# Logits in four equal pieces and a fixed plan of what runs between the groups of an attention sum

One core of a Trainium2 chip (trn2). The metric is the device time of one execution in microseconds (us), the median of the runs in the chip's fast state. "Slot" is the kernel's unit of work: one tile of 128 nodes in one of two steps. In the views of the profile PE is TensorE (PEld its weight loads), DVE is VectorE, ACT is ScalarE, POOL is GpSimd and SP is the engine that issues most transfers; L625 is line 625 of that kernel. A line `A <- B` among the waits says that A waited for B.

## The reference

Rows `x` (3327 x 256) are normed and rectified to `h`. Two steps then run an attention whose weights are cut to a nucleus (the largest probabilities that together reach 0.9) beside a diffusion over a sparse adjacency matrix; the result is normed again and added to `x`.

```python
R = S + jnp.eye(N); R = R / R.sum(-1, keepdims=True)
for n in range(STEPS):                      # 2
    A = _top_p_attention(Xa, W1, W2, W3)    # softmax(q k^T), cut to top_p, rows sum to 1
    Xf = R @ Xf
    Xa = A @ Xa
    Z = Z + Xf @ U1[n].T + Xa @ U2[n].T
h = X + Z
return (h - mu) / jnp.sqrt(var + LN_EPS) * ln_g + ln_b
```

## The kernel before

It is software-pipelined: in iteration `i`, tile `i-1` is summed with its attention weights, tile `i` gets its threshold (`settle`), tile `i+1` its first estimates (`first`, in step 1 also `second`), tile `i+2` its logits (`weights`). The sum over 26 blocks is done in seven groups; `fill(k)` puts other work between the groups.

```python
def weights(step, t, qT, ms, fill):                    # cut
    w = HALF * P                                       # 1664: two halves of the keys, 64 rows each
    for n, c in enumerate(range(0, w, 512)):           # pieces 512, 512, 512, 128
        if n >= 2: fill()
        wd = min(512, w - c)
        pl = ps_l.tile([P, 2, 512], F32, ...)
        for a in range(2):                             # both halves of the row groups
            PE.matmul(pl[:, a, :wd], qT[p, :], keys[step][p]...[:, c : c + wd], ...)
        # ACT takes exp out of PSUM: one instruction for 512, two for the last piece

def attend(r, xa, dst, n, fill):                       # cut
    eT = turn(0)                                       # 4 transposes on PE, copy eT on ACT
    for k, j0 in enumerate(starts):                    # 7 groups
        nxt = turn(starts[k + 1]) if ... else None
        fill(k)
        for j in ...: PE.matmul(pa, eT[:, j, :], xa[:, j0 + j, :D], ...)
        eT = nxt

def packed(t, over):                                   # cut: lists of adjacency blocks
    pb = ps_t.tile(...); PE.matmul(pb[:, 0, :1], upto, over, ...)
    V.tensor_copy(ls[:, LIST:], pb[:, 0, :1])          # VectorE frees PSUM

def finish(t, y1, xa2):                                # cut: end of step 1
    V.tensor_tensor(y, y1, xa2, ALU.add)
    mean, rstd = mean_rstd(y)                          # stats on VectorE, rstd on POOL (G)
    V.tensor_scalar(y, y, mean, rstd, ALU.subtract, ALU.mult)

for i in ...:                                          # the slot, cut
    settle(step, i, ...)
    qT, ms = project(step, i + 2)
    def fill(k):
        run(work, 2)                                   # diffusion, first step's ends
        if k in (1, 3): next(meas, None)               # first estimates
    attend(...)
    if step == 1: second(...)
    live[step, i + 2] = weights(...)                   # all logits after the sum
    if step == 0: listed(i + 3); packed(i + 2, ...); gathered(i + 1, ...)   # lists last
    else: xg[i + 1] = fetched(vx, i + 1, D)            # 5 gathers, issued by POOL
```

## Time and profile before

| | before |
|---|---|
| median of its fast runs on the chip of the first comparison | 1726.17 us (1721.45 to 1728.4) |
| profiled span | 1725.2 us |
| slot in step 0 while lists are searched (13 slots, the 5th to the 18th) | 34.60 us |
| slot in step 0 after that (8 slots) | 32.82 us |
| slot in step 1 (the last 17) | 26.34 us |

A slot is measured from one start of the nucleus sum's first pass (`w`, L625; L629 after the change, one a slot) to the next. Of the page of before, the busy totals (part 1), then TensorE, VectorE and granted clock in 40 slices (part 2, one digit per 43 us):

```profile
PE 1481.4 (86%) x6923; PEld 1121.1 (65%) x6923; DVE 1272.9 (74%) x3936; ACT 1103.3 (64%) x2836; POOL 769.3 (45%) x1124
...
PE   5766998899998999999999966988898898988985
...
DVE  4249877777777666466557139889999999999993
...
PEclk8657999889988998998999977989998998989988
```

TensorE fills the first half (step 0), VectorE the second (step 1). The clock row reads 8 as often as 9 in step 0. Sums over two stretches of step 0 give it a number. The columns are stretch, length, busy time with count of PE, PEld, DVE, ACT, POOL, then granted clock, DMA share, GB/s:

```profile
300.00:700.00 400.00, 369.96 (x1664) 274.14 (x1661) 282.21 (x947) 250.84 (x633) 178.86 (x236) 0.88 0.38 109
700.00:933.00 233.00, 216.90 (x1035) 164.28 (x1034) 135.86 (x446) 152.34 (x388) 105.09 (x135) 0.93 0.19 52
```

PE is busy for 92 and 93% of the two stretches, but at 0.88 and 0.93 of its clock.

### The profile page before, as it was taken

The page shows a single profiled execution, that of the slowest core. Times are in us where ns is not written, and L with a number is a line of the kernel's source. Part 1 is how long each engine was busy: PE and PEld are TensorE (multiplying, and loading weights), DVE is VectorE, ACT ScalarE, POOL GpSimd, SP SyncE. Part 2 cuts the span into 40 slices and gives each one's busy share as a digit, 9 for nine tenths or more (in the row PEclk, how much of TensorE's full clock was granted, in tenths as well). Part 3 has the DMA queues.
Part 4 walks back from the last instruction along what each step waited for, and adds up shares of the span by engine and source line. Part 5 has one row for each costly group of instructions (what it writes and reads, how often), then busy time and mean ns, then how long its engine had stood idle before and what let it go on. Part 6 is the DMA issues. An engine that isn't in the chain of part 4 may idle for free.

```text
span 1725.2 us, 23597 instructions
## 1 busy us (share of the span) xinstructions
PE 1481.4 (86%) x6923; PEld 1121.1 (65%) x6923; DVE 1272.9 (74%) x3936; ACT 1103.3 (64%) x2836; POOL 769.3 (45%) x1124
## 2 busy tenths in 40 slices
PE   5766998899998999999999966988898898988985
PEld 4634666667666776776777834666676676766765
DVE  4249877777777666466557139889999999999993
ACT  5376665566566656756765387577686776777751
POOL 6541334543444345435535183456543443436421
PEclk8657999889988998998999977989998998989988
DMA  7541444444444411212212230021221221212210
GB/s 218 152 133 47 125 133 119 129 134 136 119 129 131 113 47 51 63 41 56 58 47 62 59 107 16 21 65 44 71 65 52 65 61 53 71 48 67 71 46 12
DMA packets 86458, 139.62 MB, mean 81 GB/s; under 512 B 14737, under 2 KB 49296, under 8 KB 86320
## 3 DMA queue, kind: packets, MB, share of 16 engines
q1 hardware_dynamic: 67168, 93.76, 17.8%
q0 software_dynamic: 16640, 42.69, 9.6%
q10 hardware_dynamic: 2512, 1.57, 0.3%
q8 instruction: 57, 0.93, 0.2%
q14 instruction: 81, 0.66, 0.1%
HBM read 114.10 MB, written 23.87 MB: 80 GB/s over the span
## 4 chain that ended last, share of the span: by engine, by line
DVE 49%; PE 29%; ACT 11%; issue 4%; DMA 2%; POOL 2%; another core or an unknown queue 1%; SPq 0%; POOLq 0%; ACTq 0%; DVEq 0%
DVE cand L629 12%; PE pa L695 11%; DVE w L625 10%; DVE e L646 6%; DVE jv L594 5%; PE pt L685 5%; DVE cand L636 4%; DVE bb L634 4%; PE pl L526 3%; ACT ja L565 3%; PE pz L778 2%; DVE fm L707 2%; ACT eT L687 1%; DMA at<-in_adj 1%
## 5 line engine op out<-in xcount | busy, mean ns | idle before, releaser
L695 PE MATMUL pa<-x,eT 128*128 128x256 f32 x1352 | 359.4, 404 | 0.0
L687 ACT COPY eT<-pt 128x512 f32<-128x512 f32 (+1 forms) x364 | 198.5, 551 | 240.4 <-PE pt L685 185.1
L526 PE MATMUL pl<-k,qT 64*128 64x512 f32 (+1 forms) x832 | 257.2, 647 | 98.0 <-ACT e L530 78.4
L695 PE MATMUL pa<-xw,eT 128*128 128x256 f32 x1352 | 329.7, 389 | 5.7 <-ACT eT L687 5.7
L565 ACT ACTIVATE ja<-e,g 128x3328 uint8<-128x3328 f32 x104 | 319.6, 3073 | 0.0
L695 PEld LDWEIGHTS pa<-x,eT 128*128 128x128 f32 x1352 | 269.0, 205 | 40.2 <-ACT eT L687 0.2
L695 PEld LDWEIGHTS pa<-xw,eT 128*128 128x128 f32 x1352 | 251.0, 194 | 48.3 <-ACT eT L687 16.1
L685 PE MATMUL pt<-ident,e 128*128 128x128 f32 x1352 | 237.6, 303 | 38.0 <-DVE e L646 25.3
L685 PEld LDWEIGHTS pt<-ident,e 128*128 128x128 f32 x1352 | 183.1, 155 | 106.5 <-DVE e L646 29.9
L629 DVE MAX8 cand<-w 128x8 f32<-128x168 f32 (+1 forms) x1040 | 250.1, 315 | 0.6
L526 PEld LDWEIGHTS pl<-k,qT 64*128 64x128 f32 x832 | 91.3, 220 | 225.7 <-ACT e L530 117.4
L625 DVE SCALAR_TENSOR_TENSOR w<-e,g 128x3328 f32<-128x3328 f32 x52 | 194.7, 3743 | 1.5
L646 DVE SCALAR_TENSOR_TENSOR e<-e,rec 128x3328 f32<-128x3328 f32 x52 | 191.7, 3686 | 4.4 <-DVE rec L644 3.3
L756 POOL DMA_INDIRECT xg<-hx,index x130 | 158.9, 1223 | 79.7 <-PE pr L764 48.6
L530 ACT ACTIVATE e<-pl 128x1024 f32<-128x1024 f32 x156 | 158.3, 1018 | 34.0 <-PE pl L526 33.2
L756 POOL DMA_INDIRECT xg<-vx,index x130 | 154.2, 1186 | 41.6 <-issue 40.9
L707 DVE TENSOR_REDUCE fm<-at 128x4 f32<-128x512 f32 (+1 forms) x182 | 115.5, 639 | 72.9 <-DMA at<-in_adj 72.5
L764 PE MATMUL pr<-xg,ac 128*128 128x257 f32 (+1 forms) x520 | 149.8, 407 | 7.7 <-DMA xg<-hx,index 3.6
L746 POOL DMA_INDIRECT ac<-in_adj,index x130 | 123.8, 953 | 50.5 <-issue 37.4
L473 POOL TENSOR_TENSOR gsum<-gsum,gt 64x65 f32<-64x65 f32 x52 | 16.7, 320 | 267.1 <-ACT gt L472 266.8
L440 POOL TENSOR_SCALAR rstd<-mv 128x1 f32<-128x1 f32 x52 | 21.5, 416 | 211.6 <-DVE g L606 135.8
L764 PEld LDWEIGHTS pr<-xg,ac 128*128 128x128 f32 x520 | 98.3, 209 | 22.5 <-issue 7.0
(200 smaller groups left out, 2212.9 us busy)
## 6 DMA issues: line engine op xcount, KB each, us to landing
at<-in_adj SPq DMA_DIRECT2D x156, 256.0 KB
cx<-ac SPq DMA_DIRECT2D x26, 384.0 KB
ac<-cx SPq DMA_DIRECT2D x26, 384.0 KB
hx<-x SPq DMA_DIRECT2D x26, 128.5 KB
x<-in_x SPq DMA_DIRECT2D x13, 256.0 KB
at<-in_adj SPq DMA_DIRECT2D x26, 128.0 KB
xr<-in_x SPq DMA_DIRECT2D x26, 128.0 KB
vx<-sv SPq DMA_DIRECT2D x26, 128.0 KB
```

Of the source, the lines that this page charges most:

```text
L526: PE.matmul(pl[:, a, :wd], qT[p, :], keys[step][p].rearrange("p a b -> p (a b)")[:, c : c + wd], start=True, stop=True)
L530: S.activation(e.rearrange("p (a n) -> p a n", a=2)[:, :, c : c + wd], pl[:, :, :wd], AF.Exp, accum_out=za[:, n : n + 1])
L565: S.activation(ja, e, f, bias=col(9), scale=-1.0, accum_out=oa[:, k : k + 1])
L625: V.scalar_tensor_tensor(w, e, col(16), e, ALU.is_lt, ALU.mult, accum_out=d2)
L629: V.max(cand[:, 8 * s : 8 * s + 8], w[:, s * SEG : min(NP, (s + 1) * SEG)])
L646: V.scalar_tensor_tensor(e, e, at(1), e, ALU.is_ge, ALU.mult, accum_out=ra)
L685: PE.transpose(pt[:, j, :], e[:, (j0 + j) * P : (j0 + j + 1) * P], ident)
L687: S.copy(eT[:, :w, :], pt[:, :w, :])
L695: PE.matmul(pa, eT[:, j, :], xa[:, j0 + j, :D], start=j0 + j == 0, stop=j0 + j == NT - 1)
L707: V.tensor_reduce(fm[:, j0 : j0 + n], at[:, :n], AX.X, ALU.max, apply_absolute_value=True)
L756: G.indirect_dma_start(out=xg[:, k, :w], out_offset=None, in_=rows, in_offset=bass.IndirectOffsetOnAxis(ap=index[:, t, k : k + 1], axis=0))
L764: PE.matmul(pr[:, :w], ac[:, k, :], own if k == KT - 1 else xg[:, k, :w], start=k == 0, stop=k == KT - 1)
```

## The change

The intent: keep TensorE supplied with matmuls whose results nobody needs at once. The logits come in four equal pieces, and each piece, each list matmul and each part of the first step's ends stands at a fixed place between the groups of the sum. The two list matmuls leave PSUM (the matmul results' memory) by ACT and no longer by VectorE.

```diff
+CUT = 4
-    def weights(step, t, qT, ms, fill):
+    def weights(step, t, live):
+        qT, ms = project(step, t)
+        yield
-        for n, c in enumerate(range(0, w, 512)):
-            if n >= 2:
-                fill()
-            wd = min(512, w - c)
+        wd = w // CUT
+        for n in range(CUT):
+            c = n * wd
...                                       # a yield after each piece
-        V.tensor_copy(ls[:, LIST:], pb[:, 0, :1])
+        S.copy(ls[:, LIST:], pb[:, 0, :1])
...
+        lo = small.tile([P, n + 1], F32, tag="lo", name="lo", bufs=2)
+        S.copy(lo, po[:, 0, : n + 1])     # VectorE then reads lo instead of po
...
+    PLAN = (("wmsss", "lsss", "ewl", "mweel", "weel", "wee", "ee"),    # step 0
+            ("wms", "lss", "w", "mw", "ws", "wss", ""))                # step 1
+            # m: first estimates, w: project, then a piece of logits, s: diffusion,
+            # e: ends of step 0, l: lists (step 0) or load and gathers (step 1)
             def fill(k):
-                run(work, 2)
-                if k in (1, 3):
-                    next(meas, None)
+                for c in PLAN[step][k]:
+                    next(work[c], None)
-            run(meas, 3)
-            if step == 1 and valid(i + 1):
-                second(live[step, i + 1])
+            for c in "mwsel":
+                run(work[c], 99)
+                if c == "m" and step == 1 and valid(i + 1):
+                    second(live[step, i + 1])
```

More of the change, by code (lines that the diff above doesn't have):

```diff
@@ L512, in project @@
         return qT, ms
-    def weights(step, t, qT, ms, fill):
+    def weights(step, t, live):
+        qT, ms = project(step, t)
+        yield
         e = epool.tile([P, NP], F32, tag="e", name="e")
-        za = small.tile([P, 5], F32, tag="za", name="za")
+        za = small.tile([P, CUT + 1], F32, tag="za", name="za")
         G.memset(e[:, N:NP], 0.0)
         w = HALF * P
-        for n, c in enumerate(range(0, w, 512)):
-            if n >= 2:
-                fill()
-            wd = min(512, w - c)
+        wd = w // CUT
+        for n in range(CUT):
+            c = n * wd
             pl = ps_l.tile([P, 2, 512], F32, tag="pl", name="pl")
@@ L528, in weights @@
                           start=True, stop=True)
-            if wd == 512:
+            if n < CUT - 1:
                 S.activation(e.rearrange("p (a n) -> p a n", a=2)[:, :, c : c + wd], pl[:, :, :wd],
                              AF.Exp, accum_out=za[:, n : n + 1])
+                yield
             else:
-                S.activation(e[:, c : c + wd], pl[:, 0, :wd], AF.Exp, accum_out=za[:, 3:4])
-                S.activation(e[:, w + c : N], pl[:, 1, : wd - 1], AF.Exp, accum_out=za[:, 4:5])
+                S.activation(e[:, c:w], pl[:, 0, :wd], AF.Exp, accum_out=za[:, n : n + 1])
+                S.activation(e[:, w + c : N], pl[:, 1, : wd - 1], AF.Exp, accum_out=za[:, n + 1 :])
         g = small.tile([P, 20], F32, tag="g", name="g")
@@ L555, in weights @@
             S.activation(col(10), col(9), AF.Identity, scale=col(5), bias=con(0))
-        return dict(e=e, g=g, col=col, Z=Z)
+        live[step, t] = dict(e=e, g=g, col=col, Z=Z)
     def first(step, r):
@@ L735, in gathered @@
         PE.matmul(po[:, 0, : n + 1], oh, ls[:, DIRECT:], start=True, stop=True)
+        lo = small.tile([P, n + 1], F32, tag="lo", name="lo", bufs=2)
+        S.copy(lo, po[:, 0, : n + 1])
         nth = small.tile([P, 1], F32, tag="nth", name="nth")
-        V.tensor_scalar(nth, po[:, 0, n : n + 1], -1.0, part, ALU.mult, ALU.add)
+        V.tensor_scalar(nth, lo[:, n:], -1.0, part, ALU.mult, ALU.add)
         of = small.tile([P, LIST], F32, tag="of", name="of", bufs=2)
-        V.scalar_tensor_tensor(of[:, :n], place[:, :n], nth, po[:, 0, :n], ALU.is_equal, ALU.mult, accum_out=nth)
+        V.scalar_tensor_tensor(of[:, :n], place[:, :n], nth, lo[:, :n], ALU.is_equal, ALU.mult, accum_out=nth)
         V.tensor_scalar(index[:, t, DIRECT:], nth, -1.0, float(NONE), ALU.mult, ALU.add)
@@ L833, in run, with spread @@
             next(work, None)
-    def side(step, t):
-        if step == 0 and valid(t - 1):
-            yield from first_end(t - 1, *live.pop(("r", t - 1)))
-            yield
-        if not valid(t):
-            return
+    def spread(step, t):
         rr = rrs[:, t : t + 1]
@@ L858, in side, with index_next, refetch @@
         live["f", t] = s1
+    def index_next(t):
+        if valid(t + 3):
+            over[t + 3] = listed(t + 3)
+        yield
+        if valid(t + 2):
+            oh[t + 2] = packed(t + 2, over.pop(t + 2))
+        yield
+        if valid(t + 1):
+            ac[t + 1] = gathered(t + 1, oh.pop(t + 1))
+            xg[t + 1] = fetched(hx, t + 1, D + 1)
+    def refetch(t):
+        if valid(t + 1):
+            ac[t + 1] = adjp.tile([P, KT, P], F32, tag="ac", name="ac", bufs=2)
+            nc.sync.dma_start(ac[t + 1].rearrange("p k r -> p (k r)"), cx[t + 1])
+            xg[t + 1] = fetched(vx, t + 1, D)
+        yield
+    PLAN = (("wmsss", "lsss", "ewl", "mweel", "weel", "wee", "ee"),
+            ("wms", "lss", "w", "mw", "ws", "wss", ""))
     for step in range(2):
@@ L862, in guess_graph_layer @@
         for i in range(-3, NT + (1 if step else 2)):
+            none = iter(())
+            t = i - 1
             if valid(i):
                 settle(step, i, live[step, i])
-            meas = first(step, live[step, i + 1]) if valid(i + 1) else iter(())
-            if valid(i + 2):
-                qT, ms = project(step, i + 2)
-            t = i - 1
-            work = side(step, t) if valid(t) or t == NT else iter(())
+            work = dict(
+                m=first(step, live[step, i + 1]) if valid(i + 1) else none,
+                w=weights(step, i + 2, live) if valid(i + 2) else none,
+                s=spread(step, t) if valid(t) else none,
+                e=first_end(t - 1, *live.pop(("r", t - 1))) if step == 0 and valid(t - 1) else none,
+                l=index_next(i) if step == 0 else refetch(i),
+            )
             def fill(k):
-                run(work, 2)
-                if k in (1, 3):
-                    next(meas, None)
+                for c in PLAN[step][k]:
+                    next(work[c], None)
             if valid(t):
@@ L882, in guess_graph_layer @@
                 del live[step, t]
-            run(meas, 3)
-            if step == 1 and valid(i + 1):
-                second(live[step, i + 1])
-            if valid(i + 2):
-                live[step, i + 2] = weights(step, i + 2, qT, ms, lambda: run(work, 1))
-            run(work, 99)
+            for c in "mwsel":
+                run(work[c], 99)
+                if c == "m" and step == 1 and valid(i + 1):
+                    second(live[step, i + 1])
             if valid(t):
@@ L893, in guess_graph_layer @@
                     finish(t, live.pop(("f", t)), xa)
-            if step == 0:
-                if valid(i + 3):
-                    over[i + 3] = listed(i + 3)
-                if valid(i + 2):
-                    oh[i + 2] = packed(i + 2, over.pop(i + 2))
-                if valid(i + 1):
-                    ac[i + 1] = gathered(i + 1, oh.pop(i + 1))
-                    xg[i + 1] = fetched(hx, i + 1, D + 1)
-            elif valid(i + 1):
-                ac[i + 1] = adjp.tile([P, KT, P], F32, tag="ac", name="ac", bufs=2)
-                nc.sync.dma_start(ac[i + 1].rearrange("p k r -> p (k r)"), cx[i + 1])
-                xg[i + 1] = fetched(vx, i + 1, D)
         prove(step)
```

## The prediction

> **What bounds the kernel now.** I read the page's busy shares first, then the spacing of one instruction that runs once a slot, then sums over stretches inside one slot, then the timeline of TensorE where it stands idle, then the waits.
>
> The program is two steps of 26 slots; one slot handles one tile of 128 nodes. The instruction L625 (first pass of the nucleus sum on VectorE) runs once a slot, so its starts clock the slots. In the timeline they stand at 154.0 us (step 0, third slot) and 933.1 us (the last of step 0), 23 slots in 779 us. The first 15 of these take 34.4 us each: there VectorE also searches the adjacency for the lists (L707), about 11 tiles a slot. The last 8 take 32.8 us. In step 1 nearly all take 26.4 us (1201.3 to 1675.7).
>
> Step 0 is TensorE's. The sums over stretches of one slot (704.1 to 736.0) show how it loses time; columns are stretch, length, busy time and count of PE, PEld, DVE, ACT, POOL, then the granted clock, DMA share and GB/s:
>
> ```profile
> 704.10:713.30 9.20, 9.18 (x44) 6.69 (x42) 9.10 (x27) 2.63 (x5) 2.70 (x5) 1.00 0.08 21
> 713.30:717.10 3.80, 1.75 (x12) 1.36 (x13) 3.56 (x19) 1.81 (x9) 2.88 (x4) 1.00 0.20 52
> 717.10:722.00 4.90, 4.89 (x17) 3.33 (x18) 4.83 (x10) 3.84 (x19) 4.41 (x4) 0.65 0.26 70
> 722.00:736.00 14.00, 14.00 (x76) 11.30 (x75) 1.83 (x11) 12.83 (x25) 5.25 (x10) 1.00 0.22 71
> ```
>
> PE is full except for 3.8 us in which it is idle for 2.05 us; in the 4.9 us after that the clock granted is 0.65, which costs (1 - 0.65) x 4.9 = 1.7 us more. The timeline of PE there:
>
> ```profile
> 713.64 0.49 PE L526 MATMUL pl<-k,qT 64*128 64x128 f32 x4 [0.36 <-issue]
> 714.06 0.38 PE L724 MATMUL pb<-over,upto 128*128 128x1 f32 x2
> 714.30 0.37 PE L735 MATMUL po<-lists,oh 128*128 128x13 f32 x2
> 716.35 0.48 PE L492 MATMUL pq<-qry,w2d 64*128 64x128 f32 x2 [1.67 <-DVE lists L725]
> ...
> 717.67 1.46 PE L526 MATMUL pl<-k,qT 64*128 64x512 f32 x2
> ...
> 722.89 1.12 PE L526 MATMUL pl<-k,qT 64*128 64x512 f32 x2
> ```
>
> The list matmuls pb and po take both buffers of the PSUM pool for transposes. VectorE frees pb by a copy of 0.14 us (L725), but that copy stands behind eight-maximum rounds in VectorE's queue, so the next user (pq) waits 1.67 us. Also, the two halves of one logits piece (L526) are issued 5 us apart: one half alone takes 1.12 us at full clock, while four such pairs issued together (711.29, eight instructions) take 1.99 us.
>
> What a slot costs when nothing stands in its way is seen in the drain of step 0, where two attention slots run without logits, projection and lists:
>
> ```profile
> 940.80:961.70 20.90, 20.90 (x113) 18.06 (x112) 13.16 (x47) 6.07 (x15) 11.38 (x11) 1.00 0.27 73
> ```
>
> From 940.9 to 962.9 that is 22.0 us, PE full, full clock. Step 1 is VectorE's:
>
> ```profile
> 1227.90:1254.30 26.40, 22.57 (x105) 17.37 (x104) 25.12 (x71) 19.30 (x51) 10.57 (x19) 0.87 0.22 61
> ```
>
> VectorE is busy for 25.1 of 26.4 us. The 1.3 us left lie between the mask of e (L646) and the next L625: a wait on POOL for rstd (0.57 us) and a wait for ACT's exp L609 at the end of the chain that follows d1.
>
> **What the Trainium skill says.** "TensorE: Matmul & The Clock Gate", Part 1: the clock is either full or half, and falls to half after an idle window of about 3.4 us. The trace agrees in part: single microseconds of the slot show 1.00 or 0.50, and the drop follows a stretch that was only 46% busy, not one fully idle. The same page, Part 3: matmuls with few contraction rows in distinct row groups run at once; the trace agrees (1.99 us for eight against 1.12 us for two). "PSUM — Partial Sum Buffer", "Engine vs sequencer instructions": ScalarE and VectorE queues are strict FIFO; the 0.14 us copy that arrives 1.7 us late agrees. "Perfetto Trace Analysis", "Tensor Engine Instruction": the end of a matmul is an estimate. I therefore count PE by start-to-start times.
>
> **The change, part by part.** (1) Logits in four pieces of 416 instead of 512, 512, 512, 128. The matmul count stays 16 a slot; 1664 columns a half as before. ACT's exits: before 3 x 1.02 + 2 x 0.27 us, after 3 of 832 and 2 of 416 elements, by the same slope about 3 x 0.86 + 2 x 0.5: nothing either way. The instruction order of the changed kernel keeps both halves of each piece together in step 0, which saves most of one half, about 0.7 us of PE a slot. (2) pb and po leave PSUM by ACT: two copies of about 0.2 us more for ACT, 0.14 us less for VectorE; the 1.67 us wait goes, replaced by waits on ACT's queue. (3) The fixed plan: logits pieces, list matmuls and the first step's ends now stand between groups of pa matmuls; the long stretch at the slot's end where PE had only logits and list matmuls, each needing an exit, is gone.
>
> PE's floor in step 0: 22.0 us of the drain slot, plus logits 4 pairs x 0.81 us (1.99 / 2 pieces x 416 / 512) = 3.2, plus pq 0.7 and pb, po 0.2: 26.1 us. I then walked the new order of ACT and PE through one slot with the durations above. ACT starts two passes ja of 3.07 us (L565) early in the slot; the copies eT stand between and behind them. PE has two turns of e and five adjacency matmuls for the first pass and then waits about 1 us; it waits some 0.5 us for pb's buffer and 0.4 us for the first transposes of the next slot. Sum of stalls 1.9 us, none longer than 1.5 us, so I expect no half clock. A late slot is then 28.0 us (ACT is busy for about 22 of it, VectorE for 19.3).
>
> In the first 15 slots VectorE is busy for 26.1 us, and the adjacency tiles come through two buffers (L707 waits on its DMA 30 us in 180 to 500). Five or six of these reductions still stand in a row behind the mask of e, about 2 us apart when the load sets the pace, 0.6 us when not: some 4 us idle. These slots then become VectorE's, at about 30.2 us.
>
> Step 0: 15 x (34.4 - 30.2) + 8 x (32.8 - 28.0) = 63 + 38 = 101 us. Step 1: VectorE's work stays. The wait on POOL's rstd now lies between eight-maximum instructions and shrinks; in every second slot jv (L594) moves behind the mask, so that the ACT chain L596 to L609 is partly exposed (0.3 us). I put the slot at 25.7 us: 0.7 x 24 = 17 us. Start, drain and change of step have the same work: 0. Total 118 us, 1725 - 118 = about 1608 us.
>
> **The rivals.** A: ACT becomes step 0's bound. It is strict FIFO, its work per slot grows to 22 us, and every exit of PE (eT, logits, lists, pz) stands in that queue; a copy behind ja waits up to 3.3 us. For it: "ACT eT L687 <- PE pt L685" shows ACT and PE already hand over to each other. If each slot loses 2 us more and the clock drops again (1.7 us), step 0 gains only 101 - 23 x 3.7 = 16 us: about 1690 us. Against: at most 79% busy. B: the early slots stay bound by the list search and its DMA: VectorE was idle 8 us there already, partly on loads. Then the 63 us become perhaps 15: 1655 us. C: step 1 gets worse, since jv behind the mask exposes a whole ACT chain and logits exits L533/L534 can stand ahead of L609: plus 0.5 us a slot, 1637 us. D: better than thought: PE at its floor of 26.1 us with VectorE hiding the loads (27.5 us early), step 1 at VectorE's 25.1 us: 104 + 54 + 31 = 189 us less, 1536 us.
>
> **Range and chances.** All but a full A leave a gain above 2% (below 1691 us). A in part with B gives about 1665; half of D about 1572. Predicted 1608 us, range 1570 to 1660 us, faster 0.94, same 0.05, slower 0.01.
>
> **What would show it.** Right: L625 of step 0 spaced 30 us and then 28 us; "PE pq <- DVE lists" gone; clock near 1.00 in late step 0 slots; the two halves of a logits piece always adjacent. In step 1 VectorE over 97% busy, slot 25.7 us. Wrong: waits of PE on ACT's eT or lists copies above 3 us a slot, half clock in each slot (rival A); early slots still at 33 us with L707 waiting on DMA (B); in step 1 VectorE waiting on ACT's L609 for over 1 us in every second slot (C).

## The result

After: median 1645.95 us (1645.22 to 1652.66), before 1726.17 us on the same chip; ratio 0.9547, 95% interval 0.9515 to 0.9579. A ratio is the mean time of one kernel's fast runs over that of the other's runs of the same rounds, so it is not quite the ratio of the medians quoted. Before's median depends on the chip (1697.58, 1702.0 and about 1725 us on those used), so totals are compared below only through ratios to before on the same chip. Stages are set side by side across chips; their slots vary less.

Stages of the profiled executions, in us:

| | start to 5th slot | 13 slots of step 0 | 8 slots of step 0 | change of step | first 8 slots of step 1 | last 17 slots | tail |
|---|---|---|---|---|---|---|---|
| before | 220.8 | 449.8 | 262.6 | 92.5 | 202.2 | 447.8 | 49.5 |
| after | 223.7 | 395.8 | 228.4 | 96.5 | 208.9 | 448.1 | 49.5 |
| gain | -2.9 | 54.0 | 34.2 | -4.0 | -6.7 | -0.3 | 0 |

The sum is 74.3 us, the difference of the spans (1725.2 and 1650.8). Step 0 gave 88 us, everything else gave back 14. The mean of the last 17 slots hides two opposite changes: the first 16 of them take 26.06 us each where they took 26.35, a gain of 0.3 us a slot, and the very last takes 31.1 us where it took 26.2, a loss of 4.9 us. The page of after, parts 1 and 2, the rows of before:

```profile
PE 1424.6 (86%) x6923; PEld 1076.9 (65%) x6923; DVE 1252.1 (76%) x3910; ACT 1113.0 (67%) x2888; POOL 846.3 (51%) x1124
...
PE   5764998989989999999999758897989888998894
...
DVE  4346887887887877667671399878899999999983
...
PEclk9656999999999999999999879998999999999998
```

PE does the same 6923 instructions in 57 us less: the clock row is 9 in every slice of step 0 once it has started (the fifth slice on). VectorE's row in step 1 has eights where that of before has nines. The sums over step 0 of after, in the columns of before:

```profile
300.00:650.00 350.00, 327.57 (x1656) 250.43 (x1655) 279.51 (x927) 247.83 (x641) 192.04 (x235) 0.97 0.43 126
650.00:848.00 198.00, 191.31 (x992) 146.77 (x990) 132.43 (x433) 147.34 (x386) 116.56 (x133) 1.00 0.21 60
```

Late in step 0 PE is 97% busy at full clock. The timeline of PE in one such slot of after (start, duration, line, output<-inputs; in brackets idle time before it and what ended it) shows what stands where the long stretch of lists and logits stood:

```profile
741.30 1.90 PE L699 MATMUL pa<-x,eT 128*128 128x256 f32 x8
743.03 0.38 PE L689 MATMUL pt<-ident,e 128*128 128x128 f32 x2
743.34 0.97 PE L529 MATMUL pl<-k,qT 64*128 64x416 f32 x4
744.24 1.13 PE L797 MATMUL pw<-u,xT 128*128 128x256 f32 x4
...
753.21 0.48 PE L493 MATMUL pq<-qry,w2d 64*128 64x128 f32 x2 [0.41 <-ACT eT L691]
...
765.04 0.39 PE L739 MATMUL po<-lists,oh 128*128 128x13 f32 x2 [0.74 <-ACT eT L691]
```

Each logits piece (L529) has both halves together (four instructions, 0.97 us). Before pq PE waits 0.41 us where it waited 1.67 us, and the longest wait of this slot is 0.74 us (0.9 us in all late slots).

The waits of VectorE in step 1 (960 to 1590 us; total, times, longest) tell where step 1 lost, first before (of its waits only the one for rstd):

```profile
DVE y L804 <- POOL rstd L441: 11.8, 20, 0.7
```

and after:

```profile
DVE y L810 <- POOL rstd L442: 37.8, 23, 7.5
DVE g L618 <- ACT g L613: 3.3, 3, 2.4
DVE jv L598 <- ACT g L578: 2.7, 3, 1.5
```

The wait for `rstd`, the reciprocal deviation that POOL works out for the final norm, has tripled (over the whole run it is 15.8 us before and 42.7 us after, the figures in the expectations below). It occurs in step 1 alone. The other waits of before in this window belong to the end of its step 0 or, 9.3 us of them, to its first slots of step 1 (for ACT's g and xa), and are left out. The wait is uneven: 17.8 us stand in the first eight slots and 3.9 us in the last one (in part past this window); from 1205 to 1570 us it is 0.53 and 1.74 us in turn, 1.1 us a slot against 0.58 us before.

### The profile page after: what moved, and what is told of

Read it like the earlier page. It is cut to its first block, busy times and chain, and to the rows that moved or that the text cites. A ratio compares the mean times of both kernels' runs of the same rounds, so it can differ in the third digit from the quotient of the medians.

```text
span 1650.8 us, 23620 instructions
## 1 busy us (share of the span) xinstructions
PE 1424.6 (86%) x6923; PEld 1076.9 (65%) x6923; DVE 1252.1 (76%) x3910; ACT 1113.0 (67%) x2888; POOL 846.3 (51%) x1124
## 4 chain that ended last, share of the span: by engine, by line
DVE 33%; PE 29%; ACT 10%; POOL 8%; DMA 6%; issue 5%; SPq 0%; POOLq 0%; DVEq 0%; ACTq 0%
PE pa L699 15%; DVE cand L633 7%; POOL xg L762 7%; DVE e L650 6%; DMA at<-in_adj 6%; PE pl L529 4%; DVE w L629 4%; ACT ja L569 3%; PE pt L689 3%; DVE jv L598 3%; DVE fm L711 3%; DVE bb L638 2%; DVE cand L640 2%; PE pz L784 2%; PE pr L770 1%
## 5 line engine op out<-in xcount | busy, mean ns | idle before, releaser
L699 PE MATMUL pa<-xw,eT 128*128 128x256 f32 x1352 | 357.2, 412 | 6.4 <-ACT eT L691 6.4
L689 PE MATMUL pt<-ident,e 128*128 128x128 f32 x1352 | 208.8, 282 | 35.6 <-DVE cum L652 17.8
L529 PE MATMUL pl<-k,qT 64*128 64x416 f32 x832 | 209.8, 587 | 8.9 <-ACT e L533 7.9
L762 POOL DMA_INDIRECT xg<-vx,index x130 | 178.6, 1374 | 59.8 <-issue 33.1
L752 POOL DMA_INDIRECT ac<-in_adj,index x130 | 173.6, 1336 | 48.4 <-issue 27.4
L762 POOL DMA_INDIRECT xg<-hx,index x130 | 135.2, 1040 | 88.7 <-PE pr L770 58.3
L533 ACT ACTIVATE e<-pl 128x832 f32<-128x832 f32 x156 | 134.2, 860 | 36.4 <-PE pl L529 25.4
L770 PEld LDWEIGHTS pr<-xg,ac 128*128 128x128 f32 x520 | 92.4, 191 | 65.5 <-issue 35.2
L630 POOL TENSOR_SCALAR need<-rec,d 128x1 f32<-128x1 f32 x52 | 20.2, 389 | 189.0 <-DVE w L629 175.3
L529 PEld LDWEIGHTS pl<-k,qT 64*128 64x128 f32 x832 | 66.9, 195 | 54.8 <-issue 34.2
L598 DVE SCALAR_TENSOR_TENSOR jv<-e,g 128x3328 f32<-128x3328 f32 x26 | 96.2, 3700 | 3.9 <-ACT g L578 3.9
```

The source lines that it names most:

```text
L529: PE.matmul(pl[:, a, :wd], qT[p, :], keys[step][p].rearrange("p a b -> p (a b)")[:, c : c + wd], start=True, stop=True)
L689: PE.transpose(pt[:, j, :], e[:, (j0 + j) * P : (j0 + j + 1) * P], ident)
L699: PE.matmul(pa, eT[:, j, :], xa[:, j0 + j, :D], start=j0 + j == 0, stop=j0 + j == NT - 1)
L752: G.indirect_dma_start(out=ac[:, k, :], out_offset=None, in_=rows, in_offset=bass.IndirectOffsetOnAxis(ap=index[:, t, k : k + 1], axis=0), ...
L762: G.indirect_dma_start(out=xg[:, k, :w], out_offset=None, in_=rows, in_offset=bass.IndirectOffsetOnAxis(ap=index[:, t, k : k + 1], axis=0))
L770: PE.matmul(pr[:, :w], ac[:, k, :], own if k == KT - 1 else xg[:, k, :w], start=k == 0, stop=k == KT - 1)
```

## The experiments

Four questions: which part carries step 0's gain; whether the early slots are now held by the adjacency loads; why step 1 did not gain; whether a better version follows. The first four kernels ran on one chip (before: 1702.0 us), the next four on another (1724.46), the last four on a third (1697.58).

### One part alone, one part undone

**The list copies on ACT alone**, in the kernel before:

```diff
-        V.tensor_copy(ls[:, LIST:], pb[:, 0, :1])
+        S.copy(ls[:, LIST:], pb[:, 0, :1])
         # and po through lo = S.copy(po), as in the change
```

> The kernel before with only the list copies moved to ACT; logits and order of program as before. Theory P (the plan carries the gain of step 0, because it takes away the stretch without pa matmuls and with it the half clock; the list copies are only needed within it): the wait of pq on VectorE's copy (24 us in all) goes, but the stretch stays and pq waits for ACT instead; 1700 to 1720 us. Rival L (the 0.14 us copy behind VectorE's queue was the cause of both the idle time and the half clock): most of the step-0 gain of 88 us appears, below 1665 us.

Measured 1744.8 us, ratio 1.0255 (1.0222 to 1.0289): slower, and outside what either theory expected. Slots of step 0 are 35.03 and 33.88 us. Two of PE's waits between 700 and 826 us, three to four slots, say what became of the 1.67 us:

```profile
PE pl L526 <- ACT qT L496: 3.6, 3, 1.2
PE pq L492 <- ACT lists L725: 2.1, 4, 0.5
```

The wait of pq is down to 0.5 us, and the logits behind it now wait 1.2 us for qT, which is in ACT's queue: the same 1.7 us under another name. The clock over the eight late slots is 0.90, against 0.92 before. That the slot is a further 1 us longer is left without a proven cause.

**The equal pieces alone**, in the kernel before:

```diff
-        for n, c in enumerate(range(0, w, 512)):
+        wd = w // CUT
+        for n in range(CUT):
+            c = n * wd
...
-            wd = min(512, w - c)
-            if wd == 512:
+            if n < CUT - 1:
```

> The kernel before with only the logits cut into four equal pieces, at their old place. Both P and L: nothing clear, 1715 to 1735 us; the fourth piece now costs a full pair where the 128-piece was short, the halves are still issued apart. Rival S (the size of the pieces carries part of the gain): 1705 us or less.

Measured 1662.82 us, ratio 0.9770 (0.9733 to 0.9806), as rival S expected. Slots of step 0 are 32.46 and 30.38 us, 2.1 and 2.4 us less than before, and slots of step 1 are 25.65 us. The costliest matmuls of PE late in step 0 (count, then busy time and mean ns of one), before:

```profile
L695 PE MATMUL pa<-x,eT 128*128 128x256 f32 x374 | 100.1, 405 | 0.0
L526 PE MATMUL pl<-k,qT 64*128 64x512 f32 (+1 forms) x108 | 35.2, 587 | 2.5 <-issue 2.5
L685 PE MATMUL pt<-ident,e 128*128 128x128 f32 x186 | 32.6, 301 | 2.1 <-DVE lists L725 1.7
```

and with equal pieces alone:

```profile
L697 PE MATMUL pa<-x,eT 128*128 128x256 f32 x364 | 89.0, 382 | 0.0
L528 PE MATMUL pl<-k,qT 64*128 64x416 f32 x108 | 31.1, 704 | 0.0
L687 PE MATMUL pt<-ident,e 128*128 128x128 f32 x182 | 29.3, 285 | 0.9
```

A slot has 16 logits matmuls, so they fell from 16 x 35.2 / 108 = 5.2 us to 16 x 31.1 / 108 = 4.6 us: 0.6 us, close to the 0.7 us predicted. (Busy time counts overlapping instructions once; the mean of one does not, and is no measure here.) A slot's 52 pa matmuls, though, are 23 ns shorter each, 1.2 us, and its 26 transposes 16 ns each, 0.4 us, as a rough figure since these means overlap too. Together that is 2.2 of the 2.4 us. These are unchanged instructions, so part of it is the clock: over the eight late slots it is 0.92 before and 0.95 with equal pieces, (1 - 0.92) x 32.8 = 2.6 us and (1 - 0.95) x 30.4 = 1.5 us a slot, which accounts for 1.1 of these 1.6 us; the rest is open. What the half clock does is seen in the same kernel's timeline, at the one long stall that is left in the slot:

```profile
705.52 1.67 PE L528 MATMUL pl<-k,qT 64*128 64x416 f32 x8
707.12 0.38 PE L726 MATMUL pb<-over,upto 128*128 128x1 f32 x2
707.36 0.37 PE L737 MATMUL po<-lists,oh 128*128 128x13 f32 x2
709.52 0.48 PE L493 MATMUL pq<-qry,w2d 64*128 64x128 f32 x2 [1.79 <-DVE lists L727]
...
711.53 3.14 PE L528 MATMUL pl<-k,qT 64*128 64x416 f32 x8
```

The same eight matmuls take 1.67 us ahead of the 1.79 us stall and 3.14 us after it. So the pieces bring both halves together and shorten the half-clock time, but they do not remove the wait on VectorE's copy.

**The list copies undone**, all else as in the changed kernel (`S.copy` back to `V.tensor_copy`, VectorE reads `po`):

> The changed kernel with the list matmuls leaving PSUM by VectorE again. Theory P: the wait on VectorE returns inside the plan, one or two waits of up to 2 us a slot in step 0 and perhaps the half clock: 1665 to 1690 us. Rival L: the whole step-0 gain is lost, 1700 us or more. If under 1655 us, the ACT copies were not needed at all.

Measured 1628.89 us, ratio 0.9573 (0.9542 to 0.9605); slots 30.56 and 27.90 us, clock 0.97 and 1.00. Nothing is lost without the ACT copies: the returning waits that theory P expected (1665 to 1690 us) did not come.

**The pieces undone**, in the changed kernel:

```diff
-            c = n * wd
+            c = 512 * n
+            wd = min(512, w - c)
```

> The changed kernel with pieces of 512, 512, 512 and 128 in the same plan. Theory P: 1645 to 1655 us, since each place in the plan still has a pair of adjacent halves. Rival S: 1665 us or more.

Measured 1678.64 us, ratio 0.9871 (0.9837 to 0.9906), in rival S's range and not in theory P's. Slots of step 0 are 31.73 and 28.88 us at the same clock as the change (0.97 and 1.00), slots of step 1 are 27.18 us. So the plan takes the half clock away from the late slots without the pieces, as it did without the copies (it was not run without both, and its own parts were not tried one by one), and the pieces add to it: in the plan, as against 512, 512, 512, 128, they are worth about 1.3 us in an early slot and 0.8 us in one of step 1. Pieces alone and plan without pieces give 2.3% and 1.3%, the two together 3.8% on a chip of like time (0.9621, below). The totals hide where each acts. The 21 slots of step 0 are 69 us shorter with the plan and no equal pieces, 48 us with the pieces alone and 88 us with both; but the plan without the pieces loses 14 us in the last 17 slots of step 1 and 7.5 us at the change of step.

### Are the early slots bound by loads?

The list search was made to read two pieces of the adjacency again and again that are loaded once (the result is wrong, relative error 0.238; the search does the same work):

```diff
-            at = adjp.tile([P, AD, P], F32, tag="at", name="at", bufs=2)
-            nc.sync.dma_start(at[:, :n], adj[t, :, j0 : j0 + n, :])
+            at = held[(j0 // 4) % 2]        # two tiles, loaded at t == 0
-        V.memset(fm[:, t : t + 1], 0.0)
+        V.memset(fm[:, 12:], 0.0)
```

> The changed kernel, wrong on purpose: the list search reads two adjacency pieces that were loaded once, for all tiles; same VectorE instructions, no loads. Theory D (the first 14 slots of step 0 are bound by VectorE with its waits for these loads, 4.4 us a slot, as I predicted for them): those slots fall from 30.4 to about 28 us, 25 to 35 us less in all, 1611 to 1621 us. Rival (PE and ACT bound these slots too): under 10 us.

Measured 1622.39 us, ratio 0.9402 (0.9356 to 0.9447) where the change had 0.9547 on a like chip; the time is just above theory D's 1611 to 1621 us. Of the slots only the early ones moved, 30.44 to 28.81 us; the late ones are 28.78 us (28.55 us in the change). The wait that went, VectorE's in the changed kernel between 300 and 600 us (ten slots):

```profile
DVE fm L711 <- DMA at<-in_adj: 48.9, 35, 2.5
```

4.9 us of wait a slot was worth 1.6 us of time, because PE's own 28.8 us then bind: from 300 to 650 us PE is busy for 338 of 350 us at clock 1.00 (327.57 us at 0.97 with the loads). PE was held up as well. With the loads it waits 16.9 us ahead of the list matmul pb between 300 and 600 us, at most 3.5 us at a time, and five stretches at half clock, of 3.4 to 6.8 us, follow; without the loads both are gone. That is 13 x 1.6 = 21 us which the change leaves on the table.

### Why did step 1 not gain?

The wait that grew is VectorE's, ahead of the normed y. POOL's timeline in one regular slot of the changed kernel:

```profile
1331.90 2.98 POOL L762 DMA_INDIRECT xg<-vx,index  x1 [1.65 <-PE pr L770]
1335.18 0.95 POOL L762 DMA_INDIRECT xg<-vx,index  x1 [0.31 <-issue]
1336.44 0.95 POOL L762 DMA_INDIRECT xg<-vx,index  x1 [0.30 <-issue]
1337.69 3.63 POOL L762 DMA_INDIRECT xg<-vx,index  x1 [0.30 <-issue]
1341.63 0.95 POOL L762 DMA_INDIRECT xg<-vx,index  x1 [0.30 <-issue]
1342.67 0.26 POOL L630 TENSOR_SCALAR need<-rec,d 128x1 f32<-128x1 f32 x1
1343.01 0.23 POOL L441 TENSOR_SCALAR rstd<-mv 128x1 f32<-128x1 f32 x1
1343.33 0.57 POOL L442 TENSOR_TENSOR rstd<-rstd,half 128x1 f32<-128x1 f32 x1
```

and VectorE's beside it:

```profile
1330.26 3.67 DVE L598 SCALAR_TENSOR_TENSOR jv<-e,g 128x3328 f32<-128x3328 f32 x1
1336.82 3.69 DVE L629 SCALAR_TENSOR_TENSOR w<-e,g 128x3328 f32<-128x3328 f32 x1
...
1341.57 0.17 DVE L440 BATCH_NORM_AGGREGATE mv<-st 128x2 f32<-128x6 f32 x1
1343.93 0.42 DVE L810 TENSOR_SCALAR y<-y,mv,rstd 128x256 f32<-128x256 f32 x1 [1.74 <-POOL rstd L442]
```

VectorE hands over mv at 1341.74 us; POOL is still in its gathers, which had waited for PE's pr (the diffusion matmuls that free the gathers' buffer) and of which two were stretched to 2.98 and 3.63 us beside VectorE's long two-input passes jv and w. "SBUF — State Buffer", section "Who interferes with whom", in the Trainium skill says that a VectorE instruction with two SBUF inputs contends with a GpSimd instruction that reads SBUF (a gather reads its index there); this trace agrees, with 0.95 us alone and 2.98 and 3.63 us beside such a pass. All 22 gathers of step 1 that start inside such a pass (w, jv or the mask of e) end 0.82 to 0.96 us after the pass does. In every second slot the gathers of two slots come in a row, and VectorE waits 1.74 us there and 0.53 us in the others.

Three theories were tried: F, the gathers stand ahead of rstd; J, the second pass jv moved behind the mask in every second slot; G, the logits between the groups disturb. Rival O in the next three expectations is the new order itself, J above all.

**The gathers issued after `finish`**:

```diff
-            ("wms", "lss", "w", "mw", "ws", "wss", ""))
+            ("wms", "ss", "w", "mw", "ws", "wss", ""))
...
                     finish(t, live.pop(("f", t)), xa)
+            run(work["l"], 99)              # step 1 only
```

> The changed kernel with step 1's gathers of the next tile issued after the slot's end work again, as in the kernel before; nothing else. Theory F (the missing gain of step 1, about 24 us, is the wait of VectorE's y on rstd, which now stands behind the gathers in POOL's queue: 42.7 us in the changed kernel, 15.8 before): this wait returns to 15 to 20 us and the time falls by 12 to 25 us, to 1621 to 1634 us; the uneven slots at step 1's start (up to 32.8 us) lose most of the excess. Rival O (the new order of VectorE and ACT, jv behind the mask, is the cause): within 5 us of 1646.

Measured 1647.2 us, ratio 0.9562 (0.9519 to 0.9605): no change, slot 26.34 us, which is what rival O expected. But the experiment did not do what it was built for. VectorE's wait in step 1:

```profile
DVE y L810 <- POOL rstd L442: 39.5, 24, 7.4
```

The wait is all there. Writing the gathers later did not put them later in time: POOL's queue still holds them, until PE's pr, ahead of rstd. So this run decides nothing between F and O.

**The normed y on POOL**, so that VectorE need not wait for rstd at all:

```diff
-        V.tensor_scalar(y, y, mean, rstd, ALU.subtract, ALU.mult)
+        G.tensor_scalar(y, y, mean, rstd, ALU.subtract, ALU.mult)
```

> The changed kernel with the last normalization of y (one 128x256 instruction, 0.41 us of VectorE) done by POOL, which makes rstd itself: VectorE then never waits on POOL for it, the gathers stay early. Theory F: the 42.7 us of waits and 26 x 0.4 us of VectorE work leave step 1; 1605 to 1630 us. Rival O: only the 11 us of work go, 1633 to 1640 us.

Measured 1637.24 us, ratio 0.9501 (0.9448 to 0.9555): rival O's range, not F's. The first 8 slots of step 1 take 196.5 us instead of 208.9, and the last slot 25.9 us instead of 31.1; the 16 slots between them lose, 26.44 us instead of 26.06, and the mean of the 17 stays at 26.41 us. The waits of VectorE in step 1 there:

```profile
DVE jv L598 <- ACT g L578: 13.7, 9, 3.6
DVE y L805 <- ACT xa L702: 6.5, 3, 3.4
```

A new wait took the place of rstd's: jv now comes before ACT has its limit ready (L578, the end of the first estimates), 13.7 us where it was 2.7 us. So F holds for the first eight slots and the last one; in the regular slots other waits take over, and F alone does not account for the loss.

**The old order of step 1**, with equal pieces and step 0's plan kept:

```diff
-            ("wms", "lss", "w", "mw", "ws", "wss", ""))
+            ("ss", "mss", "ss", "m", "", "", ""))
+            if step == 1: next(work["w"], None)      # project ahead of the sum
...          # the logits after second, the gathers after finish
```

> The changed kernel with all of step 1 in the order of the kernel before (projection before attention, two steps of the side work in each group, logits after the second moment, gathers last) but with four equal pieces. Theory F: as fetch_last or a little slower, 1625 to 1642 us, as step 1 returns to its 26.4 us slots and its short start. Rival O: faster than fetch_last by over 5 us.

Measured 1627.86 us, ratio 0.9446 (0.9407 to 0.9484), 1% below the change, which both F (1625 to 1642 us) and O (over 5 us below the run with the gathers issued late) had expected. Step 1's regular slots are 25.62 us, its first eight 202.6 us, its tail 47.1 us (49.5). VectorE's waits:

```profile
DVE y L810 <- POOL rstd L442: 13.5, 24, 0.6
DVE g L618 <- ACT g L613: 5.6, 2, 3.0
DVE jv L598 <- ACT g L578: 2.9, 1, 2.9
```

The rstd wait is down by 24.3 us against the change (37.8 - 13.5), and the stages from the first slot of step 1 to the end are down by 6.3 + 12.6 + 2.4 = 21.3 us; of the 12.6 us, 6.4 are the last slot alone (24.7 us, 31.1 in the change). The sizes fit, but that does not prove that this wait was the cause: this run restores the order of every engine, the logits and the diffusion too, and the run with y on POOL took the whole wait away for a gain of only 12 us in these stages. Shown is that the new order of step 1 costs this time; that the wait for rstd is all of it is not shown.

**The plan of step 1 with the diffusion early and the logits late**, so that jv comes before the mask in each slot:

```diff
-            ("wms", "lss", "w", "mw", "ws", "wss", ""))
+            ("wmss", "lss", "ssw", "mw", "w", "w", ""))
```

> The changed kernel with step 1's six adjacency matmuls all in the first three groups of the plan, each logits piece one place after; the built order then has jv before the mask of e in every slot, where the changed kernel has it behind the mask in every second slot. Logits still stand between the groups. Theory J (the step-1 plan loses because jv moves behind the mask, so that the next slot's first pass waits for the chain after it): step 1's slot returns to 25.6 to 25.8 us, 12 to 20 us less than after_again. Rival G (it loses because logits between the groups, with their exits, disturb ACT and PE): within 4 us of after_again.

Measured 1634.75 us, ratio 0.9639 (0.9616 to 0.9663); the changed kernel, run again beside it, 0.9621 (0.9595 to 0.9647): no gain, within the 4 us that rival G expected, slots of 26.63 us. J finds no support: its order is restored in each slot, and the time is not; and the wait that J names (g on ACT, L613) is 3.3 us in all in the changed kernel. The first eight slots and the last one do gain here (3.3 and 6.1 us), and the 16 between lose 0.7 us each. VectorE's waits in step 1:

```profile
DVE y L810 <- POOL rstd L442: 21.5, 24, 5.1
DVE s L858 <- PE pr L770: 17.3, 7, 3.3
DVE y L805 <- ACT xa L702: 9.5, 7, 1.4
```

With pr early, the wait for rstd falls from 37.8 to 21.5 us, which fits the chain "pr late, gathers late, rstd late". But VectorE now waits 17.3 us for pr itself and 9.5 us for xa, the end of the sum. What this says of G is indirect: some order with logits between the groups might avoid all three waits; none of those tried did.

**The changed kernel again**, as the partner on this chip:

> The changed kernel on this chip, to compare stage by stage: ratio to the kernel before within 0.951 to 0.958.

1632.4 us, ratio 0.9621, above the 0.951 to 0.958 expected: the ratio to before differs by 0.7% between two chips too, so a ratio from one chip is compared with one from another only with that doubt. Its slots are 30.71, 27.77 and 26.34 us (30.44, 28.55 and 26.36 in the first profile): late slots of step 0 differ by 0.8 us between two executions of one kernel, so that smaller differences there mean nothing.

### A better version

**Step 1 in the old order and the list copies on VectorE**, that is, equal pieces in both steps and the plan in step 0 alone:

> Step 0 by the new plan with equal pieces, the list matmuls leaving PSUM by VectorE, step 1 in the old order. If the parts add (step1_old about 1% better than the changed kernel; p3_undone 0.65 us a late slot better and shorter at the start): ratio to the kernel before 0.935 to 0.945. If they don't: 0.945 to 0.95.

Measured 1615.56 us, ratio 0.9514 (0.9493 to 0.9535), 1.1% below the changed kernel on the same chip (0.9514 / 0.9621 = 0.989). That is above both ranges expected, which were set from ratios on other chips. The old step 1 with the ACT copies kept stood at 0.9446 / 0.9547 = 0.989 to the change, so the ACT copies are worth nothing beside the plan.

**The same with y on POOL**:

> best_dve with the last normalization of y on POOL. VectorE saves 0.41 us of work and 0.59 us of waiting for rstd in each slot of step 1, where it is the bound: 15 to 25 us less than best_dve. If POOL's queue or the shared path to memory eats it: within 5 us.

Measured 1615.08 us, ratio 0.9514 (0.9491 to 0.9537): nothing more, where 15 to 25 us or, failing that, under 5 us were expected. The first 8 slots of step 1 win 6.8 us (199.7 against 206.5), the rest gives it back (25.87 us a slot against 25.63, tail 50.6 against 47.5). The trace shows a new wait in place of the one for rstd: VectorE's dr waits for POOL's need (L630), 27.8 us in 17 times from 960 to 1590 us, at most 3.7 us.

## Why the prediction was right or wrong

The median came 38 us above the 1608 us predicted and inside the range. By its own steps:

- **Slots of step 0: right.** Predicted 30.2 and 28.0 us, measured 30.44 and 28.55 (30.71 and 27.77 in the second profile). For the 21 slots from the fifth on, the predicted differences give 13 x 4.2 + 8 x 4.8 = 93 us; 88 us came. The prediction also credited two slots before the fifth; they lie in the start, which gained nothing.
- **No half clock: right in the late slots, and due to the plan.** The clock is 0.97 and 1.00 in the change and just as much with the pieces or the copies undone. The early slots keep five stretches at half clock, behind waits of PE that end late with the list search; the prediction had no stall above 1.5 us, and these reach 3.5 us.
- **List copies by ACT remove the 1.67 us wait: wrong in the credit.** The wait went, but the plan removed it; the copies alone turn it into a wait for qT (ratio 1.0255), and beside the plan they do nothing.
- **Equal pieces, 0.7 us of PE a slot: right for the logits (0.6 us), too small for the slot.** Alone they gave 2.1 and 2.4 us, in part (1.1 us of a late slot) because other matmuls then ran less at the half clock.
- **Early slots bound by VectorE and the loads: shown**, 1.6 us a slot without the loads.
- **Step 1, 0.7 us x 24 = 17 us: the term that failed.** Its first eight slots cost 6.7 us and the last 17 cost 0.3 us: 16 of these gained 0.3 us each where 0.7 was forecast, and the last one lost 4.9 us. The step that failed reads "The wait on POOL's rstd now lies between eight-maximum instructions and shrinks". It lies there, but it grew from 11.8 to 37.8 us, as POOL's gathers now come late and stand ahead of it; that the wait is the whole of the loss is not shown. "VectorE's work stays" failed too, to the good: in the 16 regular slots VectorE is busy for 24.1 us a slot and was busy for 25.0 us, and this is what left the small gain. A slot of 25.7 us is what equal pieces give in the old order (25.65 us with them alone), for a reason that was not in the prediction: there the 128x1 instruction L613 of VectorE, 0.665 us in the median of its regular slots before, takes 0.15 us (L615), which is 0.5 of the 0.64 us a regular slot gains; why it was long is not shown. So that 25.7 us is the right figure for the best order is luck. The predicted order, jv behind the mask in every second slot, was seen, but the exposed ACT chain cost little (g on ACT: 3.3 us in all), and "over 97% busy" was not met: VectorE was busy for 386.25 of the 417 us from 1153 to 1570.
- **Start and change of step, 0: measured -2.9 and -4.0 us.** The changed kernel's start was 223.7 us in one execution and 212.4 in another, so this is within what runs differ by; the change of step (96.5 and 95.0 against 92.5 us) is not explained.
- **Rivals.** A fell: PE waits for ACT's eT at most 0.9 us at a time late in step 0 (the longer waits of early slots that the profile puts down to eT went with the loads). B is true in part, the loads do hold the early slots, but at 30.4 us and not at 33. C had the right sign for step 1 by the wrong wait. D did not come about.

The ledger of the miss: 118 us predicted, 74.3 us in the profile (80 us between the medians). Step 1 fell short by 17 + 7 = 24 us, step 0 by 101 - 88 = 13 us, start and change of step by 7 us: 44 us.

## What to carry to other kernels

A matmul stream that is short of work for under 2 us at a time can pay twice, once in the wait and once in the half clock that often follows (here stalls of 1.67 us); spreading matmuls whose results nobody needs at once removed both in the late slots here, while moving a late copy to another in-order engine only renamed the wait. When a plan moves matmuls later, follow the buffers that they free: here the gathers waited for them, and a tiny POOL instruction behind the gathers held up the bounding engine. A plan that pays in the stage bound by one engine has to be tested by itself in the stage bound by another, since the best version used it in one step only.

## What the Trainium skill lacked or had wrong

- "TensorE: Matmul & The Clock Gate", Part 1, ties the half clock to an idle window of about 3.4 us. Here it followed single stalls of 1.67 and 1.79 us (with short matmuls around them): the same eight matmuls took 1.67 us ahead of such a stall and 3.14 us after it, and with no stall above 0.9 us (late slots of the change) the clock stayed at 1.00. It did not follow each time: with equal pieces alone, two of its stalls, of 1.79 and 1.86 us (at 769 and 861 us), had none behind them. The page says that short idle times between groups of matmuls can make the clock swing (its part on PSUM-queue cycling), but has no figure for a window that is only partly idle.
- "SBUF — State Buffer", section "Who interferes with whom", names the contention of VectorE's two-input instructions with GpSimd but gives no size for this case (the page has one for a plain transfer beside a `tensor_copy`). An indirect gather issued by POOL took 0.95 us alone and 2.98 and 3.63 us beside passes of 3.7 us: of the 46 in the run that start inside a pass, 44 end 0.82 to 0.96 us after it, as if they had waited for the rest of the pass.
- No page gives the time that one indirect gather of 128 rows holds POOL (the page on DMA has one figure for what GpSimd spends on emitting a transfer, for no kind in particular): 0.95 us, with 0.30 us between two of them.
